# Latent queries, keys and values turned in one pair of transposes; latent keys and values in full-height passes over zero-padded weights

## The chip, the cores and the metric

The kernel runs on one core of one Trainium2 chip. The metric is the device time of one execution in microseconds (us); lower is better. One core has the engines PE (TensorE, matrix products, with its weight loads shown as a row of their own, PEld), DVE (VectorE), ACT (ScalarE), POOL (GpSimd) and SP (SyncE, which here only issues DMA transfers). PSUM, into which PE writes, has eight banks here, each holding 128 rows of 512 float32 values. All data are float32.

## The reference

One decoder layer for 8 sequences of 256 tokens and 256 channels, in three parts, each followed by a residual sum and a layer norm:

1. an attention with 16 heads and three branches, mixed by a gate per sequence. Its latent branch is what the change touches:
```python
nq  = _rms(x @ w_cq,  g_qnorm)        # 96 latent columns, for the queries
ckv = _rms(x @ w_ckv, g_kvnorm)       # 32 latent columns, for keys and values
q_nope, q_rope = nq @ w_dq_nope, rope(nq @ w_dq_rope)
k_nope = ckv @ w_dk_nope              # 16 heads x 32
v1     = ckv @ w_dv                   # 16 heads x 32
k_rope = rope(x @ w_krope) / 16       # shared by the heads
```
   The second branch attends to 64 selected tokens, the third to all tokens with keys and values made from `x` directly.
2. a cross attention with 16 heads over a context of 256 tokens;
3. eight experts of 1024 hidden units, of which a router weights two per token; all eight are computed.

## The kernel before

**The order of the work is planned when the program is built.** The kernel is written as 34 generators ("threads", lines 1436 to 1474), each of which yields operations. `Machine.run` (line 213) keeps for every engine the time at which it comes free, for every tile when it is written and read, and for every rotating buffer when it comes free. It takes from all threads the operation that can start earliest, and among those within 0.1 us the one of lowest rank. Each operation has an assumed cost (`mm` line 273: 2 x 0.00084 us per column, divided by `share` where several matmuls lie in different row groups; `dve_us`, `act_us`, `pool_us` lines 103 to 116). The result is a fixed order of instructions on each engine; the waits between engines follow from the data. So whatever changes an assumed cost, or the number of banks or buffers that an operation takes, can change the order of everything after it. The experts (`experts`, rank 99) are what PE does when nothing else is ready.

**PSUM** is eight tiles of one bank (`mtile`, line 308). A thread waits for a free one, or claims several at once (`m.claim`).

**The latents of a sequence** (`raw` line 744, `latents` line 758). `x` is multiplied with the 128 columns of `wA`: 96 for queries, then 32 for keys and values, into `lat` (tokens x latents). POOL squares it, DVE sums it per part, POOL makes the two reciprocal roots `rs`. DVE then scales the 96 query columns in place (line 779) and writes the 32 key-value columns twice side by side into `twice` (line 782). PE turns both, in two groups of two transposes (lines 789 and 790), into two halves of one PSUM bank, `plt`. DVE takes them out with the norm's gains: `lT` (96 rows, line 792) and `lk` (64 rows: the 32 latents in rows 0 to 31 and again in rows 32 to 63, line 793).

**Latent keys and values** (`latent_pairs`, line 924) come in two threads, "kn" and "vl", each twice per sequence, for two of the four head groups at a time. `wkv` holds the weights in 64 rows: rows 0 to 31 for the even head group, rows 32 to 63 for the odd one. A kn group is two matmuls of 32 rows x 256 columns, a vl group four of 32 rows x 128 columns; those of rows 0 to 31 and those of rows 32 to 63 lie in different row groups of the array and can run beside each other. Each head group has a PSUM bank of its own, so a group claims two. Each bank is copied out by itself (line 948, to `kn` or `vl`, by whichever of DVE and ACT the plan finds free first). `first` (line 974) multiplies queries with `kn`, `products` (line 1063) takes `vl` as weights.

**Other users of what the change touches.** `project` (line 843) uses `lT` for the queries. The two-buffer tag "turn" holds what the rotary embedding's multiply writes on DVE (`turn`, line 548) until POOL has read it; `twice` uses it too. `selection` (line 654) copies the selected tokens' values from PSUM to the tile `sv` (line 717) and writes it to DRAM. `setup` (line 382) issues the first loads on SP in order: inputs, `wA`, the rotary table, `gcol`, two loads of `gkv`, then four of `wkv`. `zeros` (line 430) clears tiles on POOL at the start.

Of the kernel before, what the change touches and what calls it, by code (L numbers as in the profile page):

```python
# [13 lines left out]
ALU = mybir.AluOpType  # L14
# [5 lines left out]
H = 16  # L20
# [238 lines left out]
def decoder_layer(ctx: ExitStack, tc: tile.TileContext, a: dict, out: bass.AP):  # L259
# [48 lines left out]
    def mtile(shape, name):  # L308
        return mtile_(shape, "m", name)

    def fixed(name, shape, dtype=F32):
        return const.tile(shape, dtype, tag=name, name=name)
# [38 lines left out]
    wkw = fixed("wkw", [P, 2, NHG, 3, HG * 32])  # L351
    wks = fixed("wks", [P, 2, NHG, 3, HG * 32])

    wkv = fixed("wkv", [64, 2, 2, P])
    gkv = fixed("gkv", [64, 1])
    wkr4 = fixed("wkr4", [P, 4, HG, 32])
    wo = fixed("wo", [P, 4, C])
    xWq = fixed("xWq", [P, 2, C])
# [23 lines left out]
    def setup():  # L382
        yield from load_sequence(0)
        yield dma(wA[:, :, 0:P], kp(a["w_lora"]))
        yield dma(wA[:, :, P:], kp(a["w_gi"]))
        done.add("first weights")
        wkr = two([P, 2, ROPE], "turn", "wkr")
        yield dma(wkr, kp(a["w_krope"]))
        for j in range(HG):
            yield dma(tab[bass.ts(j, 32)], a["rope"][0:32, 1])  # L390
        done.add("tab")
        yield dma(gcol, a["g_norm"])
        for n in range(2):
            yield dma(gkv[bass.ts(n, 32)], a["g_norm"][QL:P])
        done.add("inputs")
        yield V.tensor_scalar(
            wkr4,
            wkr.rearrange("p k (i r) -> p (k i) r", r=32).unsqueeze(2).to_broadcast([P, 4, HG, 32]),
            1.0 / H,
            None,  # L400
            ALU.mult,
        )
        m.release(wkr)
        yield seen("staged", 0)
        up = a["w_up"][QL:P, 0 : 2 * H * VH].rearrange("r (v g n c) -> n v r g c", v=2, n=2, c=P)
        for n in range(2):
            for v in range(2):
                yield dma(wkv[bass.ts(n, 32), :, v], up[n, v])
        done.add("latent weights")
        yield dma(wvw, kp(a["w_winv"]))  # L410
        yield dma(wvs, kp(a["w_selv"]))
        done.add("setup")
# [15 lines left out]
        m.release(t)  # L428

    def zeros():  # L430
        yield G.memset(vs[KEEP:P, 0], 0.0)
        yield G.memset(vs[0:KEEP, 1], 0.0)
        yield seen("heads", 0, 0)
        yield G.memset(vx, 0.0)
        yield G.memset(xk, 0.0)
        yield dma(wo, a["w_proj"].rearrange("(g p) c -> p g c", p=P))
        yield from compact(xWk, "xWk", 2)
        yield dma(xWv, kp(a["xWv"]))
        done.add("ctx weights")
        yield from compact(xWq, "xWq", 0)  # L440
        yield dma(mrow, a["xb"][:, 8:9])
        yield dma(bo, a["bo"].partition_broadcast(P))
        values = a["bv"].rearrange("(g i j d) -> j i d g", i=2, j=4, d=XH)
        rows = a["xWo"].rearrange("(g i j d) c -> j i d g c", i=2, j=4, d=XH)
        for j in range(4):
            for i in range(2):
                yield dma(wos[bass.ds(32 * j + XH * i, XH)], rows[j, i])
                yield dma(bv[bass.ds(32 * j + XH * i, XH)], values[j, i])
        yield V.tensor_scalar(qb, xb[:, 0:2], 0.25, None, ALU.mult)
        yield G.tensor_scalar(xq.rearrange("p g t -> p (g t)"), mrow.to_broadcast([P, NHG * T]), FILL, None, ALU.mult)  # L450

        wide = two([P, 2, P], "turn", "wide")
        yield G.tensor_copy(wide, bv.unsqueeze(2).to_broadcast([P, 2, P]))
        pb = mtile([P, C], "pbo")
        yield group([mm(pb, wide[:, g], wos[:, g], g == 0, g == 1) for g in range(2)])
        m.release(wide)
        yield V.tensor_tensor(bo, pb, bo, ALU.add)
        m.release(pb)
        done.add("query weights")
        yield dma(wr, kp(a["Wr"]))  # L460
        yield dma(br, a["br"].partition_broadcast(P))
        yield dma(b1, a["b1"])
        yield dma(b2, a["b2"])
        done.add("router weights")
# [189 lines left out]
    def selection(s, d):  # L654
# [59 lines left out]
            ]  # L714
        )
        used(lead(s))
        sv = one([P, H * VH], "sv", "sv")
        yield copied(sv[0:rows], pv[0:rows])
        m.release(pv)
        pro[lead(s)]["sv"] = dv = kept_in_dram([P, H * VH], f"sv{lead(s)}")  # L720
# [37 lines left out]
    def latents(s, d):  # L758
        xT = xTs[s]

        yield seen("raw", s)
        lat = d["lat"]
        sq = two([P, 2, P], "turn", "sq")
        yield G.tensor_tensor(sq, lat, lat, ALU.mult)
        ms = tiny("ms", [P, 2, 2])
        rs = tiny("rs", [P, 2, 2])
        parts = ((0, QL), (QL, P))
        for w, (lo, hi) in enumerate(parts):
            yield V.tensor_reduce(ms[:, w, :], sq[:, :, lo:hi], AX.X, ALU.add)
        m.release(sq)  # L770
        for w, (lo, hi) in enumerate(parts):
            yield V.tensor_scalar(ms[:, w, :], ms[:, w, :], 1.0 / (hi - lo), RMS_EPS, ALU.mult, ALU.add)
        yield rsqrt(rs.rearrange("p a b -> p (a b)"), ms.rearrange("p a b -> p (a b)"), 4)
        lT = one([P, T], "lT", "lT")
        lk = one([64, T], "lk", "lk")
        yield m.claim(lT, lk)
        yield seen("inputs")
        twice = two([P, 2, 2, 32], "turn", "twice")
        yield V.tensor_tensor(
            lat[:, :, 0:QL], lat[:, :, 0:QL], rs[:, 0, :].unsqueeze(2).to_broadcast([P, 2, QL]), ALU.mult  # L780
        )
        yield V.tensor_tensor(
            twice,
            lat[:, :, QL:P].unsqueeze(2).to_broadcast([P, 2, 2, 32]),
            rs[:, 1, :].unsqueeze(2).unsqueeze(3).to_broadcast([P, 2, 2, 32]),
            ALU.mult,
        )
        plt = mtile([P, 2, T], "plt")
        yield group([tr(plt[0:QL, 0, bass.ts(i, P)], lat[:, i, 0:QL]) for i in range(2)])
        yield group([tr(plt[0:64, 1, bass.ts(i, P)], twice[:, i].rearrange("p n c -> p (n c)")) for i in range(2)])  # L790
        m.release(lat, twice)
        yield V.tensor_scalar(lT[0:QL], plt[0:QL, 0], gcol[0:QL], None, ALU.mult)
        yield V.tensor_scalar(lk, plt[0:64, 1], gkv, None, ALU.mult)
        m.release(plt)
        d["lT"], d["lk"] = lT, lk
        done.add(("latent", s))
        lx = one([P, 2, T], "lx", "lx")
        yield m.claim(lx)
        pk = mtile([P, 2, T], "pkr")
        for i in range(2):  # L800
            yield group(
                [
                    mm(pk[:, i], wkr4[:, 2 * k + i].rearrange("p h r -> p (h r)"), xT[:, k, :], k == 0, k == 1)
                    for k in range(2)
                ]
            )
        yield from turn([lx[:, 0], lx[:, 1]], pk, T)
        m.release(pk)
        d["lx"] = lx
        done.add(("shared", s))  # L810
# [32 lines left out]
    def project():  # L843
        for s in range(B):
            yield 2 + AHEAD * s
            d = pro.setdefault(s, {})
            for g in range(NHG):
# [69 lines left out]
                )  # L917
                yield copied(h["vw"], pv)
                m.release(pv)
                if g == NHG - 1:  # L920
                    m.release(d["lT"])
                done.add(("values", s, g))

    def latent_pairs(name):

        for s in range(B):
            yield 2 + AHEAD * s
            d = pro.setdefault(s, {})
            for g in range(2):
                yield seen("heads", s, 2 * g)  # L930
                lk = d["lk"]
                t = one([P, 2, T], name, name)
                d[name, g] = t
                ps = [mtile([P, T], "p" + name) for _ in range(2)]
                yield m.claim(t)
                yield m.claim(*ps)
                ops = []
                for n, p_ in enumerate(ps):
                    rows = bass.ts(n, 32)
                    if name == "kn":  # L940
                        ops.append((p_, wkv[rows, g, 0], lk[rows]))
                    else:
                        ops += [(p_[:, bass.ts(i, P)], lk[rows, bass.ts(i, P)], wkv[rows, g, 1]) for i in range(2)]
                if name != "kn":
                    ops = ops[0::2] + ops[1::2]
                yield group([mm(*op, share=2) for op in ops], 0.1)
                for n, p_ in enumerate(ps):
                    yield copied(t[:, n], p_)
                m.release(*ps)
                done.add((name, s, g))  # L950
                if name != "kn" and g == 1:
                    yield seen("kn", s, 1)
                    m.release(lk)


    def scores(h, d, g, st, which):
# [106 lines left out]
    def products():  # L1063
        for s in range(B):
            yield 3 + AHEAD * s
            oT = None
            for g in range(NHG):
# [2 lines left out]
                yield seen("selected values", s)  # L1070
                yield seen("values", s, g)
                yield seen("vl", s, g // 2)
                vl = pro[s]["vl", g // 2][:, g % 2].rearrange("p (i c) -> p i c", i=2)
                if g == 0:
                    oT = one([P, NHG, T], "oT", "oT")
                    yield m.claim(oT)
# [494 lines left out]
```

## Time and profile before

| | |
|---|---|
| three timed runs | 1674.11, 1671.38, 1673.97 us; median 1673.97 |
| the profiled execution's own time | 1674.96 us |
| its span, first to last instruction | 1673.2 us |
| mean granted PE clock in it | 0.986 |
| busy: PE, PEld | 1609.5 us (96%), 1320.2 us (79%) |
| busy: DVE, ACT, POOL | 1158.9 (69%), 583.8 (35%), 599.7 us (36%) |
| HBM traffic | 196 GB/s over the span |

A float32 matmul appears as two PE rows (two passes), each with a weight load; a transpose as one. A PE row's duration is the time from its start to its modelled end, and successive passes overlap, so what a pass takes from PE is read from the distance of the starts of successive rows. A line of the timeline gives the start of a run of equal instructions, the time from the first start to the last end, and their number. A line of groups gives busy time, the mean duration of one in ns, and the idle time of the engine just before them with what ended it. In a line of the table of stages, each engine's busy time in the stretch is followed by its number of instructions, then the granted clock, the DMA share and GB/s.

### The profile page before, as it was taken

How to read it: one execution, taken by the hardware profiler on the slowest of the kernel's cores; microseconds unless marked ns; L12 is line 12 of the kernel's file. 1: busy time of each engine (PE TensorE's matmuls, PEld its weight loads, DVE VectorE, ACT ScalarE, POOL GpSimd, SP SyncE). 2: the span in 40 equal slices, each digit the busy share in tenths (PEclk: the TensorE clock that was granted, in tenths of full speed). 3: DMA queues.
4: the chain of work that ended last, by engine and by line, in shares of the span. 5: the costliest groups of instructions: out<-in, count | busy, mean ns of one | idle time of the engine just before them, and what ended most of it. 6: DMA issues, size and time to landing. Idle time of an engine off the chain costs nothing.

```text
span 1673.2 us, 31920 instructions
## 1 busy us (share of the span) xinstructions
PE 1609.5 (96%) x12040; PEld 1320.2 (79%) x12040; DVE 1158.9 (69%) x2577; ACT 583.8 (35%) x2114; POOL 599.7 (36%) x795
## 2 busy tenths in 40 slices
PE   6899789999999999999999999999999999999998
PEld 4778568887887778888888688878888778888887
DVE  4968678678789874887678884688767774544333
ACT  2464543244435430434434341244435341220000
POOL 3665753253534430334235332243335332120000
PEclk8999899999999999999999999999999999999999
DMA  6311416378648675655746676566656777585552
GB/s 218 117 50 47 166 69 217 120 245 284 233 141 291 245 248 192 211 205 189 252 172 234 241 249 227 151 238 211 226 196 221 248 257 251 154 307 153 161 156 96
DMA packets 185657, 329.96 MB, mean 197 GB/s; under 512 B 13200, under 2 KB 105504, under 8 KB 178336
## 3 DMA queue, kind: packets, MB, share of 16 engines
q1 hardware_dynamic: 185504, 327.92, 57.6%
q8 instruction: 96, 1.57, 0.4%
q14 instruction: 57, 0.47, 0.1%
HBM read 237.70 MB, written 90.19 MB: 196 GB/s over the span
## 4 chain that ended last, share of the span: by engine, by line
PE 83%; issue 7%; DVE 4%; DMA 3%; POOL 1%; SPq 1%; ACT 0%; POOLq 0%; DVEq 0%; ACTq 0%
PE ph L280 23%; PE py L280 22%; PE s L280 9%; PE o L280 4%; PE pk L280 3%; PE pyo L280 3%; PE ox L280 2%; PE pv L280 2%; PE sx L280 2%; DMA xpt<-prx 1%; PE pkm L280 1%; PE pks L280 1%; PE pq L280 1%; PE pt L286 1%; PE pkr L280 1%
## 5 line engine op out<-in xcount | busy, mean ns | idle before, releaser
L280 PE MATMUL ph<-xT,w 128*128 128x256 f32 x2048 | 475.2, 382 | 3.8 <-DVE pl L98 2.6
L280 PE MATMUL py<-w,h 128*128 128x256 f32 x2048 | 471.5, 381 | 0.0
L280 PEld LDWEIGHTS ph<-xT,w 128*128 128x128 f32 x2048 | 383.8, 190 | 70.2 <-issue 16.7
L280 PEld LDWEIGHTS py<-w,h 128*128 128x128 f32 x2048 | 383.7, 190 | 59.7 <-issue 7.7
L98 ACT ACTIVATE h<-ph,b 128x256 f32<-128x256 f32 x227 | 107.5, 473 | 391.5 <-PE ph L280 340.0
L98 DVE TENSOR_SCALAR h<-ph,b 128x256 f32<-128x256 f32 x285 | 136.9, 482 | 112.5 <-PE ph L280 109.6
L98 DVE SCALAR_TENSOR_TENSOR xr<-py,rw,xr 128x256 f32<-128x256 f32 x128 | 61.2, 478 | 174.7 <-PE py L280 174.6
L98 POOL TENSOR_TENSOR prx<-prx,sumsx 128x512 f32<-128x512 f32 x128 | 130.6, 1051 | 118.8 <-DVE sumsx L98 73.2
L98 ACT ACTIVATE prx<-sx,nmx 128x256 f32<-128x256 f32 x256 | 117.0, 486 | 43.3 <-DVE nmx L98 41.9
L98 POOL TENSOR_TENSOR pr<-pr,wpr 128x256 f32<-128x256 f32 (+2 forms) x128 | 129.4, 1042 | 0.0
L98 POOL TENSOR_TENSOR rstd<-var,nhalf 128x2 f32<-128x2 f32 x24 | 17.4, 725 | 310.0 <-DVE var L98 309.9
L98 ACT ACTIVATE pl<-pl,nmpl 128x128 f32<-128x128 f32 (+1 forms) x256 | 113.1, 446 | 30.6 <-DVE nmpl L98 29.9
L98 POOL TENSOR_TENSOR kx<-turn 128x64 f32<-128x64 f32 (+1 forms) x128 | 65.3, 527 | 162.6 <-DVE turn L98 156.9
L98 ACT ACTIVATE pr<-pr,nmpr 128x128 f32<-128x128 f32 (+1 forms) x256 | 113.2, 447 | 0.0
L98 DVE TENSOR_TENSOR pr<-s,causal 128x256 f32<-128x256 f32 x128 | 74.6, 583 | 41.0 <-PE s L280 34.6
L280 PE MATMUL s<-kx,q 32*128 32x320 f32 (+1 forms) x1536 | 96.1, 390 | 0.3 <-POOL kx L98 0.3
L98 POOL TENSOR_TENSOR pl<-pl,wpl 128x512 f32<-128x512 f32 x64 | 93.1, 1475 | 2.7
L98 POOL TENSOR_TENSOR q<-turn 128x256 f32<-128x256 f32 x64 | 45.8, 735 | 134.1 <-DVE turn L98 130.8
L280 PEld LDWEIGHTS s<-kx,q 32*128 32x128 f32 x1536 | 71.2, 189 | 17.8 <-issue 7.1
L98 DVE TENSOR_REDUCE nmx<-sx 128x2 f32<-128x512 f32 x128 | 79.1, 678 | 8.5 <-PE sx L280 8.5
L98 DVE TENSOR_TENSOR pl<-s,causal 128x256 f32<-128x256 f32 x128 | 74.3, 581 | 12.6 <-PE s L280 8.6
L98 DVE TENSOR_REDUCE nmpr<-pr 128x4 f32<-128x256 f32 (+2 forms) x128 | 80.5, 673 | 0.0
(217 smaller groups left out, 2385.1 us busy)
## 6 DMA issues: line engine op xcount, KB each, us to landing
w<-in_W SPq DMA_DIRECT2D x256, 512.0 KB, 4.2
pr<-pr SPq DMA_DIRECT2D x28, 1024.0 KB, 4.1
pa<-pr SPq DMA_DIRECT2D x28, 1024.0 KB, 6.9
prx<-prx SPq DMA_DIRECT2D x28, 1024.0 KB, 5.2
xpt<-prx SPq DMA_DIRECT2D x28, 1024.0 KB, 6.5
pl<-pl SPq DMA_DIRECT2D x28, 768.0 KB, 4.9
pb<-pl SPq DMA_DIRECT2D x28, 768.0 KB, 7.2
xT<-in_xT SPq DMA_DIRECT2D x8, 256.0 KB
```

The source lines that it names most:

```text
L98: return Op(self.name, us, outs, ins, lambda: getattr(self.engine, kind)(*args, **kw))
L280: lambda: nc.tensor.matmul(out, lhsT, rhs, start=start, stop=stop, skip_group_check=share > 1),
L286: return Op("PE", 0.11, [out], [in_], lambda: nc.tensor.transpose(out, in_, ident[:n, :n]), lag=0.17)
```

## The change

- `wkv` becomes 128 rows x 1024 columns (512 for keys, 512 for values). Rows 96 to 127 hold the weights and come in one DMA; rows 0 to 95 are cleared once by POOL at the start. `gkv` and its two DMAs go.
- In `latents`, the key-value columns are scaled in place like the query columns, without doubling; both are turned together, two transposes per sequence instead of four; one DVE instruction takes all 128 rows out with the gains of both. `lT` now has 128 rows, `lk` and `twice` go. `lT` is released in the "vl" thread, after the last use in `project`.
- In `latent_pairs`, each group is two matmuls of 128 rows x 256 columns into one bank: the 96 rows of query latents meet zeros. One copy of 512 columns takes the bank out. The tile is one bank where it was two, and is no longer claimed ahead.
- `sv` moves from a tile of its own to the "turn" buffers.
- `products` takes `vl` from its new layout.

```diff
--- before.py
+++ after.py
@@ -351,8 +351,7 @@
     wkw = fixed("wkw", [P, 2, NHG, 3, HG * 32])
     wks = fixed("wks", [P, 2, NHG, 3, HG * 32])
 
-    wkv = fixed("wkv", [64, 2, 2, P])
-    gkv = fixed("gkv", [64, 1])
+    wkv = fixed("wkv", [P, 2 * H * VH])
     wkr4 = fixed("wkr4", [P, 4, HG, 32])
     wo = fixed("wo", [P, 4, C])
     xWq = fixed("xWq", [P, 2, C])
@@ -390,8 +389,6 @@
             yield dma(tab[bass.ts(j, 32)], a["rope"][0:32, 1])
         done.add("tab")
         yield dma(gcol, a["g_norm"])
-        for n in range(2):
-            yield dma(gkv[bass.ts(n, 32)], a["g_norm"][QL:P])
         done.add("inputs")
         yield V.tensor_scalar(
             wkr4,
@@ -402,10 +399,7 @@
         )
         m.release(wkr)
         yield seen("staged", 0)
-        up = a["w_up"][QL:P, 0 : 2 * H * VH].rearrange("r (v g n c) -> n v r g c", v=2, n=2, c=P)
-        for n in range(2):
-            for v in range(2):
-                yield dma(wkv[bass.ts(n, 32), :, v], up[n, v])
+        yield dma(wkv[QL:P], a["w_up"][QL:P, 0 : 2 * H * VH])
         done.add("latent weights")
         yield dma(wvw, kp(a["w_winv"]))
         yield dma(wvs, kp(a["w_selv"]))
@@ -428,6 +422,7 @@
         m.release(t)
 
     def zeros():
+        yield G.memset(wkv[0:QL], 0.0)
         yield G.memset(vs[KEEP:P, 0], 0.0)
         yield G.memset(vs[0:KEEP, 1], 0.0)
         yield seen("heads", 0, 0)
@@ -714,7 +709,7 @@
             ]
         )
         used(lead(s))
-        sv = one([P, H * VH], "sv", "sv")
+        sv = two([P, H * VH], "turn", "sv")
         yield copied(sv[0:rows], pv[0:rows])
         m.release(pv)
         pro[lead(s)]["sv"] = dv = kept_in_dram([P, H * VH], f"sv{lead(s)}")
@@ -772,27 +767,18 @@
             yield V.tensor_scalar(ms[:, w, :], ms[:, w, :], 1.0 / (hi - lo), RMS_EPS, ALU.mult, ALU.add)
         yield rsqrt(rs.rearrange("p a b -> p (a b)"), ms.rearrange("p a b -> p (a b)"), 4)
         lT = one([P, T], "lT", "lT")
-        lk = one([64, T], "lk", "lk")
-        yield m.claim(lT, lk)
+        yield m.claim(lT)
         yield seen("inputs")
-        twice = two([P, 2, 2, 32], "turn", "twice")
-        yield V.tensor_tensor(
-            lat[:, :, 0:QL], lat[:, :, 0:QL], rs[:, 0, :].unsqueeze(2).to_broadcast([P, 2, QL]), ALU.mult
-        )
-        yield V.tensor_tensor(
-            twice,
-            lat[:, :, QL:P].unsqueeze(2).to_broadcast([P, 2, 2, 32]),
-            rs[:, 1, :].unsqueeze(2).unsqueeze(3).to_broadcast([P, 2, 2, 32]),
-            ALU.mult,
-        )
-        plt = mtile([P, 2, T], "plt")
-        yield group([tr(plt[0:QL, 0, bass.ts(i, P)], lat[:, i, 0:QL]) for i in range(2)])
-        yield group([tr(plt[0:64, 1, bass.ts(i, P)], twice[:, i].rearrange("p n c -> p (n c)")) for i in range(2)])
-        m.release(lat, twice)
-        yield V.tensor_scalar(lT[0:QL], plt[0:QL, 0], gcol[0:QL], None, ALU.mult)
-        yield V.tensor_scalar(lk, plt[0:64, 1], gkv, None, ALU.mult)
+        for w, (lo, hi) in enumerate(parts):
+            yield V.tensor_tensor(
+                lat[:, :, lo:hi], lat[:, :, lo:hi], rs[:, w, :].unsqueeze(2).to_broadcast([P, 2, hi - lo]), ALU.mult
+            )
+        plt = mtile([P, T], "plt")
+        yield group([tr(plt[:, bass.ts(i, P)], lat[:, i]) for i in range(2)])
+        m.release(lat)
+        yield V.tensor_scalar(lT, plt, gcol, None, ALU.mult)
         m.release(plt)
-        d["lT"], d["lk"] = lT, lk
+        d["lT"] = lT
         done.add(("latent", s))
         lx = one([P, 2, T], "lx", "lx")
         yield m.claim(lx)
@@ -917,8 +903,6 @@
                 )
                 yield copied(h["vw"], pv)
                 m.release(pv)
-                if g == NHG - 1:
-                    m.release(d["lT"])
                 done.add(("values", s, g))
 
     def latent_pairs(name):
@@ -928,29 +912,22 @@
             d = pro.setdefault(s, {})
             for g in range(2):
                 yield seen("heads", s, 2 * g)
-                lk = d["lk"]
+                lT = d["lT"]
                 t = one([P, 2, T], name, name)
                 d[name, g] = t
-                ps = [mtile([P, T], "p" + name) for _ in range(2)]
-                yield m.claim(t)
-                yield m.claim(*ps)
-                ops = []
-                for n, p_ in enumerate(ps):
-                    rows = bass.ts(n, 32)
-                    if name == "kn":
-                        ops.append((p_, wkv[rows, g, 0], lk[rows]))
-                    else:
-                        ops += [(p_[:, bass.ts(i, P)], lk[rows, bass.ts(i, P)], wkv[rows, g, 1]) for i in range(2)]
-                if name != "kn":
-                    ops = ops[0::2] + ops[1::2]
-                yield group([mm(*op, share=2) for op in ops], 0.1)
-                for n, p_ in enumerate(ps):
-                    yield copied(t[:, n], p_)
-                m.release(*ps)
+                p_ = mtile([P, 2, T], "p" + name)
+                if name == "kn":
+                    yield group([mm(p_[:, n], wkv[:, bass.ts(2 * g + n, P)], lT) for n in range(2)])
+                else:
+                    w = wkv[:, bass.ds(H * VH + 2 * P * g, 2 * P)]
+                    yield group([mm(p_[:, i], lT[:, bass.ts(i, P)], w) for i in range(2)])
+                yield copied(t, p_)
+                m.release(p_)
                 done.add((name, s, g))
-                if name != "kn" and g == 1:
-                    yield seen("kn", s, 1)
-                    m.release(lk)
+            if name == "vl":
+                yield seen("kn", s, 1)
+                yield seen("values", s, NHG - 1)
+                m.release(lT)
 
 
     def scores(h, d, g, st, which):
@@ -1070,7 +1047,7 @@
                 yield seen("selected values", s)
                 yield seen("values", s, g)
                 yield seen("vl", s, g // 2)
-                vl = pro[s]["vl", g // 2][:, g % 2].rearrange("p (i c) -> p i c", i=2)
+                vl = pro[s]["vl", g // 2][:, :, bass.ts(g % 2, P)]
                 if g == 0:
                     oT = one([P, NHG, T], "oT", "oT")
                     yield m.claim(oT)
```

## The prediction

> **What bounds the kernel.** I read the page's busy shares first, then the table of stages, then PE's waits, then PE's timeline around the groups that change.
>
> ```profile
> PE 1609.5 (96%) x12040; PEld 1320.2 (79%) x12040; DVE 1158.9 (69%) x2577; ACT 583.8 (35%) x2114; POOL 599.7 (36%) x795
> ...
> PE 83%; issue 7%; DVE 4%; DMA 3%; POOL 1%; SPq 1%; ACT 0%; POOLq 0%; DVEq 0%; ACTq 0%
> ```
>
> PE is busy for 96% of the span and is 83% of the chain that ended last. The stages show where the rest is:
>
> ```profile
> 0.00:40.00 40.00, 24.05 (x122) 18.35 (x126) 17.85 (x54) 7.77 (x18) 15.09 (x33) 0.83 0.68 212
> 40.00:80.00 40.00, 35.32 (x310) 29.61 (x302) 36.95 (x104) 17.45 (x61) 26.38 (x41) 0.91 0.44 138
> 80.00:160.00 80.00, 76.17 (x793) 60.95 (x792) 63.70 (x159) 45.14 (x155) 50.37 (x63) 0.98 0.14 48
> 160.00:310.00 150.00, 133.94 (x1161) 106.36 (x1160) 110.53 (x263) 66.56 (x250) 72.93 (x96) 0.94 0.44 155
> 310.00:1673.00 1363.00, 1340.06 (x9667) 1104.97 (x9666) 929.86 (x2000) 446.87 (x1634) 434.94 (x562) 1.00 0.62 212
> ```
>
> In the first 310 us PE is busy for 269.5 and idle for 40.5; its clock is below 1.00 there, which costs about 0.17 x 40 + 0.09 x 40 + 0.02 x 80 + 0.06 x 150 = 21 us more. Afterwards it is idle for 22.9 us in 1363, about 6.6 of it after its last matmul. So after 310 us each added us of PE's time is an added us of the kernel; before, it is partly a matter of who waits.
>
> **The price of a pass.** The last experts give it without disturbance:
>
> ```profile
> 1569.71 7.07 PE L280 MATMUL ph<-xT,w 128*128 128x256 f32 x32
> 1576.62 0.59 PE L280 MATMUL py<-w,h 128*128 128x256 f32 x2
> ```
>
> From start to start 6.91 us for 32 passes: 0.216 us for a pass of 128 rows and 256 columns. pq, with 96 rows, has a mean duration of 394 ns against 382 for ph: I count a full-height pass at 0.216 whatever its rows. A new group, kn or vl, is 2 matmuls x 2 passes x 0.216 = **0.864 us**.
>
> **The price of the groups that go.** A kn and a vl group between full-height neighbours, and a kn group behind scores, which are in row groups themselves:
>
> ```profile
> 1236.44 0.38 PE L280 MATMUL pq<-lT,wq 96*128 96x256 f32 x1
> 1236.75 0.70 PE L280 MATMUL pkn<-lk,wkv 32*128 32x256 f32 x4
> ...
> 1237.38 1.99 PE L280 MATMUL ph<-xT,w 128*128 128x256 f32 x8
> ```
>
> ```profile
> 820.82 0.28 PE L280 MATMUL pv<-wvw,xT 128*128 128x128 f32 x1
> 821.03 0.71 PE L280 MATMUL pvl<-wkv,lk 32*128 32x128 f32 x8
> ...
> 821.67 0.48 PE L280 MATMUL ph<-xT,w 128*128 128x256 f32 x1
> ```
>
> ```profile
> 1147.30 0.61 PE L280 MATMUL s<-kn,q 32*128 32x256 f32 x8
> 1147.73 0.60 PE L280 MATMUL pkn<-lk,wkv 32*128 32x256 f32 x4
> 1148.26 1.56 PE L280 MATMUL py<-w,h 128*128 128x256 f32 x6
> ```
>
> From pq's last pass to ph it is 0.94 us; without the group it would be 0.216, so the kn group costs 0.724. The vl group costs 0.85 - 0.112 (a 128-column pass) = 0.737. Both hold a changeover: the step into row groups takes 0.309 where a pass takes 0.216. Behind scores that changeover is paid anyway (row groups to full height, median 0.304 from start to start), and the kn group costs 0.73 - 0.304 = 0.42.
>
> I went through all 32 groups in this way, by their neighbours:
> - 8 kn and 10 vl groups between full-height work: 8 x 0.140 + 10 x 0.127 = +2.4 us.
> - 3 kn groups behind scores, one between two sorts of partial passes: 4 x 0.44, less 0.02 = +1.7.
> - 2 vl groups behind column-group work (cost 0.643): 2 x 0.22 = +0.4. 2 vl groups just ahead of scores (0.45): 2 x 0.42 = +0.8.
> - Twice a kn and a vl group in a row beside scores: +0.62 and +0.65 = +1.3.
> - 2 kn groups that stalled (377 and 710 us), at the clean difference: +0.3.
> Sum **+7.0 us** (0.22 a group). If the new plan put every group between full-height work it would be 32 x 0.13 = +4.3; if beside scores, 32 x 0.44 = +14.
>
> The Trainium skill's page "TensorEngine Tiling (Array Packing)", section "Theoretical Speedup", promises up to twice the speed for a contraction of at most 64 rows, and speaks against this change: by it the groups would have cost half of 0.864, and the change would add 32 x 0.432 = 13.8 us where I have 7.0. The trace has 0.724 and 0.737 between full-height work, so I keep the rows.
>
> **Transposes.** 16 of them go, at half the distance here:
>
> ```profile
> 1216.22 0.38 PE L286 MATMUL plt<-ident,twice 128*64 128x128 f32 x2
> 1216.44 1.46 PE L280 MATMUL py<-w,h 128*128 128x256 f32 x6
> ```
>
> 0.22 us for two, 8 x 0.22 = **-1.75 us**. The remaining ones grow from 96 to 128 weight columns: their loads are 127 ns against 190 for a full one, beside a neighbour's pass; nothing counted (at most 16 x 0.06 = 1 us).
>
> **Stalls of the two-bank groups.** The kn group at 377 us took 1.65 us from its first start to the next work where 0.63 is normal; the one at 710 had its second bank late:
>
> ```profile
> 710.05 0.59 PE L280 MATMUL pkn<-lk,wkv 32*128 32x256 f32 x2
> 711.39 0.66 PE L280 MATMUL pkn<-lk,wkv 32*128 32x256 f32 x2 [0.75 <-DVE pr L98]
> ```
>
> Together 2.5 us over the clean cost. With one bank there is one wait in place of two, which may be as late. I take **-1.0**, bounds 0 and -2.5.
>
> **The start.** At 11.4 us PE waits for `lat`, then turns both halves for 0.88 us before pkr. The new order waits for the second scaling as well (about 0.1 us later: `twice` starts 0.27 after `lat`, and its half-size successor is shorter), then needs only 0.43. pkr comes 0.35 us sooner, DVE's multiply waits for it, and the top-k chain behind it on DVE holds up PE until 26.8 (6.67 us). SP drops two gkv and three wkv issues of about 0.47 us ahead of the next staged weights, 2.3 us, but those wait for buffers and the chain for DVE. I take **-0.4**, bounds 0 and -1.0.
>
> **Costed at nothing.**
> - DVE loses `lk` (0.47 us) and part of `twice`, 8 times: some 5 us of 1159, beside PE's work. It can only help.
> - Copies: two of 256 columns (0.38 each on ACT, 0.41 on DVE) become one of 512 (0.585 and 0.68). The first scores with the keys wait for it; two in a row on ACT took 0.65, so it lands no later. If both copies had run beside each other it lands 0.2 later; at worst 32 x 0.3 = 10 us, if PE had nothing else, but experts stand ready from about 250 us.
> - The clearing of `wkv`: a clear of 128 x 1024 took POOL 0.95 us; POOL sits idle for 4.64 us before 7.75. If it came later, one 0.95 us in front of `sq` would move the whole start by that.
> - `sv` in a "turn" buffer: five copies (36.7, 97.5, 303.4, 706.6, 1090.3 us), held until the write has landed, 3 us. The nearest multiply behind them comes 6.9, over 9, 7.4, over 9 and 8.7 us later. None waits in this order; in another, behind a held buffer, up to 3 us of DVE each, at most 15, which PE mostly fills.
> - `lT`'s release moves threads but has the same conditions: the next latents waited for `lk` at the same point.
>
> **The new plan.** Cheaper latents, dearer groups and half the banks change the assumed costs, so the order changes from the first sequence on. No row shows by how much. Its field is the early idle time and lost clock, 40.5 + 21 us; a fifth of the 40.5 either way, 8 us, is my bound, and its value 0, because PE's work after 310 us is full in any order.
>
> **Sum:** +7.0 - 1.75 - 1.0 - 0.4 = **+3.9 us**. Against the profiled execution's 1674.96 that is 1678.8; it lies 1.0 above the median of the runs, so I state 1674.0 + 3.9 = about **1678**.
>
> **Rivals.**
> - **Within 0.2%** (3.35 us, about what a measurement of this kernel can tell from no change). Both credits come at their ends: 7.0 - 1.75 - 2.5 - 1.0 = +1.75, **1676**. For it: the stalls are in the trace. Against: one bank can be as late as two.
> - **Faster**, by one mechanism: the early plan. A pair of groups holds one bank where it held two, and DVE has a latent step less in front of `turn`, just where PE idles for DVE (the longest waits there are 6.7 for the top-k chain, 5.2 for a layer norm, 2.7 for `lat`). If a fifth of the 40.5 + 21 us goes, -12, with +5.2 paid in passes: -7, **1667**. It decides from 3.9 + 3.35 = 7.3 us gained, an eighth of the field. Against: the two longest waits have nothing in them that the change removes.
> - **Slower by more.** The new order opens one more hole like the one at 243 us, 5.2 us for a layer norm, followed by 6.8 us at half clock (3.4 lost): 1678 + 8.6 = **1687**.
> - **The groups don't cost what I say**: were the passes not bound by their columns but by the 32 useful rows, nothing would be added and the sum would be -3, 1671. pq at 96 rows against ph at 128, 394 and 382 ns, speaks against it; it is counted with the faster case.
>
> **Chances.** Forecast 0.40; within 0.2% 0.27; slower by more 0.13; faster 0.20 (0.03 of it for the last rival). So slower by over 0.2%: 0.53, same 0.27, faster 0.20. The range takes in the bound of the plan on both sides, 1678 + 8 and somewhat more for the hole, and most of the faster case: **1667 to 1687**.
>
> **What will show it.** pkn and pvl as 4 passes each, 0.216 apart, 0.86 from start to next start, with no 0.309 step before; two plt transposes a sequence; PE busy time up by 4 to 6 us; the stage from 310 us on as full as before. I am wrong if the groups stand at another distance, or if the first 310 us differ by more than 8 us.

## The result, and the profile after

| | before | after |
|---|---|---|
| median of the timed runs | 1674.04 us (4 runs) | 1697.47 us (4 runs) |
| ratio, 95% interval | | 1.0145, 1.013 to 1.016 |
| span of the profiled execution | 1673.2 us | 1694.7 us |
| PE busy / idle (span less busy) | 1609.5 / 63.7 us | 1623.2 / 71.5 us |
| mean granted PE clock | 0.986 | 0.981 |

The kernel became slower by 23 us, as forecast in sign, but by six times the forecast 3.9 and outside the range. Because the median of the kernel before varied from 1672.4 to 1675.1 us between the groups of runs below, I compare by ratios, each against runs of the kernel before in the same group; 0.0010 of ratio is 1.7 us.

**A new group costs what was forecast.** PE's timeline of the kernel after, a kn and a vl group between full-height passes:

```profile
1261.26 1.03 PE L280 MATMUL pkn<-lT,wkv 128*128 128x256 f32 x4
1262.12 1.03 PE L280 MATMUL pq<-lT,wq 96*128 96x256 f32 x4
1262.99 1.03 PE L280 MATMUL pvl<-wkv,lT 128*128 128x256 f32 x4
1263.85 0.81 PE L280 MATMUL py<-w,h 128*128 128x256 f32 x3
```

Each is 4 passes and 0.86 us from its start to the next start, and pq with 96 rows takes as long. The transposes came down to two a sequence, 0.22 us for the pair:

```profile
1235.83 0.38 PE L286 MATMUL plt<-ident,lat 128*128 128x128 f32 x2
1236.05 1.68 PE L280 MATMUL py<-w,h 128*128 128x256 f32 x7
```

**The rest is idle time and clock.** The same table of stages as before the change (PE's busy time is the second figure, the clock the third from the end):

```profile
0.00:40.00 40.00, 23.93 (x117) 17.84 (x118) 17.61 (x54) 7.42 (x17) 16.33 (x34) 0.83 0.69 211
40.00:80.00 40.00, 35.75 (x295) 30.13 (x296) 35.28 (x103) 16.55 (x55) 26.74 (x41) 0.91 0.47 139
80.00:160.00 80.00, 78.05 (x843) 62.91 (x841) 64.94 (x167) 50.87 (x176) 48.82 (x64) 1.00 0.12 41
160.00:310.00 150.00, 127.80 (x1058) 100.39 (x1051) 116.46 (x257) 60.82 (x226) 75.99 (x96) 0.91 0.39 135
310.00:1695.00 1385.00, 1357.66 (x9660) 1123.52 (x9658) 935.26 (x1988) 442.11 (x1607) 440.24 (x569) 0.99 0.63 211
```

Up to 160 us nothing is lost. From 160 to 310 PE is idle for 22.2 us where it was 16.1, at a clock of 0.91 where it was 0.94. From 310 on it is idle for 27.3 where it was 22.9, at 0.99 where it was 1.00. Over the whole span the clock's loss (span times what is missing to 1) is 32.2 us against 23.4. While PE idles a low clock costs nothing, so I count half of PE's busy time in the stretches at half clock: 24.5 us against 15.9. So of the span's +21.5 us, 7.8 are idle time, 8.6 the clock, and what is left, about 5, is busy time of another kind: dearer passes and whatever else PE's order adds.

The two longest new holes, in PE's timeline:

```profile
215.88 1.51 PE L280 MATMUL o<-pb,vl 128*32 128x128 f32 x16 [5.89 <-DMA pb<-pl]
...
563.25 1.51 PE L280 MATMUL o<-pa,vw 128*32 128x256 f32 x16 [7.50 <-ACT prx L98]
```

By the profile, the first waits for a transfer, the second for ACT to read scores out of their PSUM bank. ACT in its turn waited for DVE, whose timeline shows what stood in front of the reduction that ACT needed:

```profile
557.51 1.41 DVE L98 TENSOR_TENSOR_SCAN sc<-left 1x256 f32<-1x256 f32 x1
558.95 1.08 DVE L98 TENSOR_TENSOR sc<-sc,left 1x256 f32<-1x256 f32 x1
560.07 1.01 DVE L98 TENSOR_SCALAR sc<-sc 1x256 f32<-1x256 f32 x1
...
561.32 2.48 DVE L98 TENSOR_REDUCE nmx<-sx 128x2 f32<-128x512 f32 x4
```

That is the top-k chain of another sequence. None of these DVE instructions is touched by the change; only their place in the order is new.

### The profile page after: what moved, and what is told of

It is laid out like the page before. It is cut to its first block, busy times and chain, and to the rows that moved or that the text cites. A ratio compares the mean times of both kernels' runs of the same rounds, so it can differ in the third digit from the quotient of the medians.

```text
span 1694.7 us, 31673 instructions
## 1 busy us (share of the span) xinstructions
PE 1623.2 (96%) x11960; PEld 1334.8 (79%) x11960; DVE 1169.5 (69%) x2565; ACT 577.8 (34%) x2079; POOL 608.1 (36%) x803
## 4 chain that ended last, share of the span: by engine, by line
PE 79%; DVE 7%; issue 7%; DMA 4%; POOL 2%; ACT 0%; SPq 0%; POOLq 0%; DVEq 0%; ACTq 0%
PE ph L280 22%; PE py L280 21%; PE s L280 9%; PE o L280 3%; PE pk L280 3%; PE pyo L280 2%; PE pv L280 2%; PE sx L280 2%; PE ox L280 2%; PE pq L280 2%; PE pks L280 2%; PE pkm L280 1%; DMA pb<-pl 1%; DMA pl<-pl 1%; DVE left L98 1%
## 5 line engine op out<-in xcount | busy, mean ns | idle before, releaser
L280 PE MATMUL ph<-xT,w 128*128 128x256 f32 x2048 | 480.0, 383 | 0.3 <-PE o L280 0.2
L98 DVE TENSOR_SCALAR h<-ph,b 128x256 f32<-128x256 f32 x314 | 150.5, 482 | 115.2 <-PE ph L280 112.5
L98 ACT ACTIVATE h<-ph,b 128x256 f32<-128x256 f32 x198 | 94.0, 475 | 361.8 <-PE ph L280 361.3
```

The source lines that it names most:

```text
L98: return Op(self.name, us, outs, ins, lambda: getattr(self.engine, kind)(*args, **kw))
L280: lambda: nc.tensor.matmul(out, lhsT, rhs, start=start, stop=stop, skip_group_check=share > 1),
```

## The theories

**Theory A: the removed claim.** The change also drops a line that the prediction passed over: `latent_pairs` no longer claims its destination tile (`kn`, `vl`: one buffer each) before the matmuls. The vl group of 174 us is the clearest case, in PE's and in ACT's timeline:

```profile
174.36 1.03 PE L280 MATMUL pvl<-wkv,lT 128*128 128x256 f32 x4
```

```profile
217.45 0.59 ACT L98 COPY vl<-pvl 128x512 f32<-128x512 f32 x1 [0.31 <-PE o L280]
```

The product lies in its PSUM bank for 43 us, until `vl` is free. Added over all groups (first matmul to end of copy, times banks), latent groups hold banks for 584 us; it was 110. By theory A the lost bank makes the holes.

**Theory B: the order.** The change alters assumed costs, the number of banks and the claims, so the planner arranges everything anew. The order of the kernel before is better than most; the new one is just another.

**Theory D**, added after the first runs: the change's instructions cost more than their passes (operands later, `sv` in the "turn" buffers).

## Experiments: claims, costs, banks

**e1**, the change with its claim put back:

```diff
                 p_ = mtile([P, 2, T], "p" + name)
+                yield m.claim(t)
```

> The changed kernel with one line added: latent_pairs claims its destination tile (kn or vl) before it issues the matmuls, as the kernel before did. Theory A (a latent group that is multiplied before its destination tile is free keeps its PSUM bank for up to 90 us, and that lost bank makes the new holes): the loss beyond the dearer passes goes, about 16 us, time 1677 to 1682, pvl banks held about 1.7 us each in place of 31 on average. Theory B (any change of assumed costs gives a different and, by chance, worse order): the time stays within some 8 us of 1697 or goes anywhere.

Measured: 1.0135 (1.0114 to 1.0156), 1696.3 us. Latent groups hold banks for only 54 us in total, yet PE is idle for 81.3 us. Theory A misses: the claim alone brings back nothing that can be told from the change (1.0145).

**e2**, the kernel before without it:

```diff
-                yield m.claim(t)
                 yield m.claim(*ps)
```

> The kernel before with one line removed: latent_pairs no longer claims its destination tile ahead (the two banks are still claimed). No instruction differs in kind or number. Theory A: pairs of banks are held for tens of us and the kernel slows by at least the 16 us seen in the changed kernel, which holds one bank, not two: 1688 to 1710. Theory B: an order that differs by chance, within 8 us of 1674.

Measured: 1.0288 (1.0255 to 1.0321), 1721.8 us. Banks are held for 1068 us. This alone would suit theory A.

**e3**, the change with the old assumed cost:

```diff
-yield group([mm(p_[:, n], wkv[:, bass.ts(2 * g + n, P)], lT) for n in range(2)])
+yield group([mm(p_[:, n], wkv[:, bass.ts(2 * g + n, P)], lT) for n in range(2)], -0.33)
...
-yield group([mm(p_[:, i], lT[:, bass.ts(i, P)], w) for i in range(2)])
+yield group([mm(p_[:, i], lT[:, bass.ts(i, P)], w) for i in range(2)], -0.33)
```

> The changed kernel with the planner told that a latent group costs 0.53 us, as it was told before, in place of 0.86; the instructions are the same in kind and number. Theory A: banks are held as in the changed kernel, 1690 to 1702. Theory B, in the form that the dearer assumed cost spoiled the order: back to 1677 to 1682.

Measured: 1.0278 (1.0249 to 1.0307), 1721.1 us. Neither: it is 22 us above the change, with banks held as long (593 us). A cost told closer to the old one made the order worse.

**e4**, the kernel before with seven banks:

```diff
-    mtile_ = m.pool(ps, 8)
+    mtile_ = m.pool(ps, 7)
```

> The kernel before with 7 PSUM tiles in place of 8: the price of one bank missing all the time. In the changed kernel latent groups hold a bank for 584 us in total (sum over 32 groups), against some 110 before. Theory A: if 470 us of one bank cost 16 us, a bank missing for the 1400 us in which attention runs costs up to 50: 1690 to 1724. Theory B: the eighth bank is worth little, within 8 us of 1674.

Measured: 1.0207 (1.0186 to 1.0228), 1708.3 us, inside theory A's bounds. But by now everything that was altered had cost 23 to 48 us, whatever it was. That called for two other kinds of run: one that changes the order and nothing else, and one that changes everything but the order.

## Experiments: the order alone, and everything but the order

**j1 and j2**: the kernel before, instruction for instruction, with one assumed cost altered.

```diff
-                yield group([mm(*op, share=2) for op in ops], 0.1)
+                yield group([mm(*op, share=2) for op in ops], 0.12)
```

> The kernel before with the planner told that a latent group costs 0.02 us more (0.55 in place of 0.53). Not an instruction differs in kind or number; the order is the same up to about 300 us. Theory B, with the order of before a rare good one: 1680 to 1710. If plans scatter evenly about 1674: within 8 us of it on either side. Theories A and D: 1674, since no bank is held and nothing is added.

```diff
-.get(kind, 0.15 + 0.00106 * n)
+.get(kind, 0.151 + 0.00106 * n)
```

> The kernel before with the planner told that every plain VectorE instruction costs 0.001 us more. Not an instruction differs in kind or number; the order differs from about 60 us on. Theory B: 1680 to 1720. Theories A and D: 1674.

Measured: j1 1.0135 (1.0113 to 1.0158), 1698.4 us; j2 1.0189 (1.0162 to 1.0216), 1707.1 us. Nothing was added, latent groups hold banks no longer than before (96 us each), and the loss is about as large as the change's or larger. j1's stages, of which the first 300 us have the old order:

```profile
160.00:310.00 150.00, 132.87 (x1147) 105.62 (x1149) 108.97 (x256) 65.16 (x243) 73.00 (x96) 0.93 0.44 152
310.00:1703.00 1393.00, 1355.49 (x9684) 1114.01 (x9672) 953.37 (x2017) 438.32 (x1618) 442.33 (x569) 0.98 0.62 208
```

The scores that start at 304.2 us in the kernel before start at 305.7 here, 1.5 us later; the whole span is 29.3 us longer. After 310 us PE is idle for 37.5 us (22.9 before) and the clock is at 0.98. Over the whole span PE's idle time grew by 15.3 us and the clock's loss while PE is busy by 13.8 (29.7 against 15.9), which together make the 29.

**j3**: as j2, downwards (0.149).

> The kernel before with the planner told that every plain VectorE instruction costs 0.001 us less; no instruction differs in kind or number. Theory B, order of before a rare good one: 1685 to 1715, like the two others. If orders scatter evenly about 1674, this is the one that should come out below it.

Measured: 1.0119 (1.0092 to 1.0145), 1693.8 us. Three altered orders, all slower by 20 to 32 us: the order of the kernel before is no middle of its scatter.

**x1 and x2**: the change in the old order. The planner's picks for the kernel before (which thread, on which engine) were recorded and imposed on the changed kernel:

```diff
-            t, _, op, th = min(picks, key=lambda x: x[0])
+            who, engine = divmod(order.pop(), 5)
+            th = next(th for th in threads if th[3] == who)
+            ops = th[2] if isinstance(th[2], tuple) else (th[2],)
+            op = next(o for o in ops if o.engine == names[engine])
```

x1 keeps two banks and two copies per group:

> The changed kernel's latents, weights and full-height passes, but with the two banks, the two copies and the claims of the kernel before, and with every engine's instructions in the recorded order of the kernel before (only what the change removes is left out of it; vl in 8 passes of 128 columns, 0.112 us each). Theory A, now in doubt: nothing to lose here, 1678 to 1681. Theory B (the plan's order is the loss, not any instruction): 7.0 + 0.5 - 1.75 = +5.8, so 1678 to 1681. Theory D (the change's own instructions cost more than their passes: later operands, sv in the turn buffers): 1688 or more.

x2 is the whole change but for the claims: the destination tile is claimed again, and a second bank is claimed and left unused.

```diff
-                p_ = mtile([P, 2, T], "p" + name)
+                p_, spare = mtile([P, 2, T], "p" + name), mtile([P, T], "spare")
+                yield m.claim(t)
+                yield m.claim(p_, spare)
```

> All of the change (one bank per group, one copy, sv in the turn buffers), with every engine's instructions in the recorded order of the kernel before. The destination tile is claimed ahead and a second, unused bank is claimed with the group, so that the claims fall where they fell. Theory B: +5.2 for passes and transposes, less the stalls, 1676 to 1681. Theory D: 1688 or more.

Measured: x1 1.0030 (1.0016 to 1.0044), x2 1.0029 (1.0012 to 1.0045), 1679.7 and 1679.5 us. The change, in the old order, costs 4.9 us (2.0 to 7.5). From x2's table of stages:

```profile
160.00:310.00 150.00, 134.11 (x1149) 107.32 (x1152) 110.39 (x258) 67.74 (x250) 74.80 (x98) 0.94 0.45 156
310.00:1679.00 1369.00, 1343.94 (x9634) 1112.02 (x9623) 929.11 (x1995) 446.97 (x1618) 435.47 (x562) 1.00 0.62 211
```

Idle time and clock are close to those of the kernel before: 15.9 us at 0.94 and 25.1 at 1.00, where it had 16.1 and 22.9. Theory D falls. Theory B holds: same instructions, old order +5, new order +24. Since x2 also claims its destination tile, the strictest comparison is with e1, which does so too: 1.0029 in the old order, 1.0135 in a new one, 18 us for the order alone.

**d1**: x2 with each latent group multiplied twice.

```diff
-yield group([mm(p_[:, n], wkv[:, bass.ts(2 * g + n, P)], lT) for n in range(2)])
+yield group([mm(p_[:, n], wkv[:, bass.ts(2 * g + n, P)], lT) for n in range(2)] * 2)
```

> The change in the order of the kernel before (as x2), with every latent key and value group multiplied twice over into the same bank: 128 full-height passes more, 0.216 us each, and the order of no engine altered. If PE is the bound wherever these groups stand: 1679.5 + 27.6 = 1707. If half of them fell into time in which PE waits anyway: about 1693. It prices a pass in place, and with it the term +7.0 - 1.75 of the prediction.

Measured: 1.0185 (1.0156 to 1.0213), 0.0156 above x2: 26 us for the expected 27.6. PE's busy lines of x2 and of d1:

```profile
PE 1612.0 (96%) x11960; PEld 1327.8 (79%) x11960; DVE 1155.4 (69%) x2561; ACT 582.9 (35%) x2090; POOL 601.0 (36%) x796
```

```profile
PE 1639.4 (96%) x12088; PEld 1352.0 (80%) x12088; DVE 1155.6 (68%) x2561; ACT 583.1 (34%) x2090; POOL 601.2 (35%) x796
```

128 passes more, 27.4 us more of busy time, 0.214 each: the passes lie on the path that sets the end.

## Experiments: is the claim worth anything?

Since orders scatter, one run each way can't tell. The same two alterations (0.151 and 0.149) gave more draws of the change (k1, k2), of the change with its claim (c1, c2) and of the kernel before without it (c3, c4).

> The changed kernel with the planner told that every plain VectorE instruction costs 0.001 us more. Theory B: another draw of the same scatter as the order of before with the same alteration (1707) or the claimed and re-costed versions of the change (1696, 1721): 1690 to 1725. If the change itself spoiled the order by its structure, its draws lie above those of the kernel before by more than the 5 us of its passes.

> The changed kernel with the planner told that every plain VectorE instruction costs 0.001 us less. As for the alteration upwards: 1690 to 1725 by theory B, its mean with the others above that of the altered orders of the kernel before by about 5 us.

> The changed kernel with the destination tile claimed ahead (as e1), and the planner told that a plain VectorE instruction costs 0.001 us more. If held banks cost, the draws with the claim (1696 and these two) lie below those without it (1697, 1721, 1716, 1704; mean 1710) by 10 us or more. If they cost nothing that shows, this is one more draw from 1690 to 1722.

> As the run with 0.001 us more, with 0.001 us less: below 1700 on average with the two others if held banks cost; 1690 to 1722 if not.

> The kernel before without the claim of the destination tile (as e2), and the planner told that a plain VectorE instruction costs 0.001 us more. If pairs of banks held for tens of us cost, the draws without the claim (1722 and these two) lie above those with it (1698, 1707, 1694; mean 1700) by some 20 us. If not: 1690 to 1722, mean near 1700.

> As the run with 0.001 us more, with 0.001 us less: about 1720 on average with the two others if held banks cost; near 1700 if not.

| draws | ratios to the kernel before | mean | banks held by latent groups |
|---|---|---|---|
| before, altered (j1, j2, j3) | 1.0135, 1.0189, 1.0119 | 1.0148 | 93 to 96 us |
| before, no claim (e2, c3, c4) | 1.0288, 1.0190, 1.0409 | 1.0296 | 961 to 1217 us |
| change with claim (e1, c1, c2) | 1.0135, 1.0118, 1.0138 | 1.0130 | 54 to 58 us |
| change (after, e3, k1, k2) | 1.0145, 1.0278, 1.0249, 1.0177 | 1.0212 | 467 to 629 us |

The intervals are about 0.002 to 0.003 either way, for c1 to c4 (fewer timed runs) 0.0035 to 0.008. Without the claim the mean is higher by 0.0148 (25 us) in the kernel before and by 0.0082 (14 us) in the change. With three or four draws each, which spread by 0.002 to 0.022, this points to a price of going without the claim, on the average over orders; that the held bank is the reason is argued, not shown, since every draw is also another order. Nor does it show a price for the particular order of the changed kernel, which lies only 0.0010 above e1. And between the change with its claim and the altered orders of the kernel before there is no difference at all (1.0130, 1.0148): the 5 us that the change costs in the old order drown in the scatter.

## Why the prediction was right in sign and wrong in size

- **Price of a pass, and transposes, -1.75**: right. The new groups stand 0.86 us apart, the pairs of transposes 0.22, and d1 prices a pass at 0.214 busy.
- **Price of the groups that go, in the +7.0**: too low between full-height work, so the term was some 2 us too large. I took 0.724 and 0.737 us, up to the start of the first pass behind the group. But where row groups end, the second full-height pass comes 0.320 us after the first, not 0.216 (76 cases, 0.319 to 0.321), which I passed over. The kernel before and x2 have the same work around a kn group:

```profile
1235.69 1.13 PE L280 MATMUL pq<-lT,wq 96*128 96x256 f32 x4
1236.75 0.70 PE L280 MATMUL pkn<-lk,wkv 32*128 32x256 f32 x4
1237.38 2.86 PE L280 MATMUL ph<-xT,w 128*128 128x256 f32 x12
1240.17 0.73 PE L280 MATMUL s<-lx,q 32*128 32x128 f32 x16
```

```profile
1241.00 1.13 PE L332 MATMUL pq<-lT,wq 96*128 96x256 f32 x4
1241.97 1.03 PE L332 MATMUL pkn<-lT,wkv 128*128 128x256 f32 x4
1242.84 2.75 PE L332 MATMUL ph<-xT,w 128*128 128x256 f32 x12
1245.52 0.73 PE L332 MATMUL s<-lx,q 32*128 32x128 f32 x16
```

From pq to the scores it is 4.48 us before and 4.52 in x2: +0.04 where I had +0.140. By the starts in the two traces, the vl groups between full-height work give +0.025 where I had +0.127. For these 18 groups that is about +0.5 us in place of +2.4, and the whole term about +5. Behind scores, my +0.44 is what the traces show.

- **Stalls of the two-bank groups, -1.0 (0 to -2.5)**: in x2 the group at 379 us takes 0.89 us from its start to the next work's, the one at 713 takes 1.20; they were 1.65 and 1.94. Less the clean costs some 2 us of stalls went, near the far end of my bounds.
- **The start, -0.4**: not there. From PE's first instruction to the end of the top-k wait it is 21.67 us before and after, and 22.3 in x2, where DVE's `lat` came later.
- **Costed at nothing** (copies, clearing of `wkv`, `sv` in "turn", `lT`): a few us at most. x1 and x2, with two copies and one, differ by 0.0001, and in the old order all of the change together costs 4.9 us; none of these was tested by itself.
- **These terms together, +3.9**: x2's +4.9 (2.0 to 7.5) lies close, but partly by luck. With the sizes measured above they come to 5 - 1.75 - 2 = about +1.3. In the profiled executions x2's span is 5.7 us longer, of which 3.2 are idle time and 1.6 the clock's loss while PE is busy, which leaves about 1. The interval begins at 2.0, so part of that idle time and clock seems to belong to x2 itself; where it comes from, no run shows.
- **The new plan, 0, at most 8 us either way**: this is the step that failed. It was about +19: the change lies 0.0116 above x2, the same work in another order and without the claim (0.0106, 18 us, for e1 with it). So of the 24 us measured, some 19 came from a term that I had set at nothing. Two things were wrong in it. I took its field to be the first 310 us, "because PE's work after 310 us is full in any order"; j1 has the old order until about 300 us and loses nearly all of its 29 us behind it. PE was full there because the order was good: in the changed kernel PE stands idle for 7.50 us ahead of `o` at 563.25 us, and the experts' next pass, `ph` at 567.30, stands behind it in the order. And I set the value to 0, as if an order were as likely to be better as worse; all thirteen altered kernels that were planned anew lie 20 to 68 us above the kernel before, none below. The field was also smaller than the 40.5 + 21 us that I named: of the 41 us at half clock in the first 310, PE was idle for 12, so the clock cost about 14 there, not 21.
- **The claim**: I listed its removal in the change and counted only the banks ("half the banks"), not how long one is held: 43 us in the case shown. The draws point to a price on average; in this order it isn't separable.
- **Rivals**: the mechanism of "slower by more" (one more hole of 5.2 us and the half clock behind it) was the right one; there were several, so 9 us was too little. "Faster" rested on DVE's relief and on freed banks in the early stage; DVE was busy for 10.6 us more after the change (in the new order it does 314 of the experts' copies `h` where it did 285), and PE's idle time rose.
- **Signs**: the groups' distance came as said. PE's busy time rose by 13.7 us where I named 4 to 6, and the stage from 310 us on was less full: the two signs that speak of the order.

What stays open: what makes the order of the kernel before so good, and which of the new order's holes carry how much of its loss. Against x2 the span is 15.8 us longer, of which 4.6 are idle time and 7.0 the clock's loss while PE is busy; some 4 us of busy time I can't assign. No version here beats the kernel before.

## What to carry to other kernels

Where a planner orders a program, price the change's instructions and the new order as two terms. The second can be measured without the change, by altering an assumed cost by a thousandth of a microsecond: if that alone moves the time by 20 us, a step of 5 us can't be judged from one build, and has to be run in the recorded old order. A claim that holds a producer back until its consumer's buffer is free looks like a cost; dropping it lets the product sit in a scarce bank (43 us in the case shown), and it is worth a test of its own. And where a group changes the array's shape, its price is read up to where the passes behind it run at their usual distance again, not to the first of them.

## What the runs showed of the hardware

A latent group in two groups of 32 rows, between full-height work, costs hardly less than the same product over 128 rows, three quarters of them zeros: about 0.83 us (kn) and 0.84 (vl) against 0.864. The step into row groups took 0.309 us, the step out 0.304 (median), and the second pass behind it came 0.320 after the first, where full-height passes stand 0.216 apart. Beside scores, which are in row groups already, a kn group cost 0.42, half of 0.864. The Trainium skill's page "TensorEngine Tiling (Array Packing)", section "Key Properties", says that a change of the tiling mode drains the engine, which agrees; the factor of two in its section "Theoretical Speedup" was reached beside other row groups, and not for groups as short as these between full-height work.

Around the two long new holes of the changed kernel, of 5.89 us up to 215.88 and of 7.50 us up to 563.25, the clock was lost as well. The stages:

```profile
215.00:221.80 6.80, 5.92 (x37) 5.08 (x38) 1.52 (x4) 2.13 (x4) 3.93 (x4) 0.50 0.21 78
...
559.70:566.50 6.80, 3.25 (x48) 2.17 (x48) 6.73 (x11) 3.76 (x16) 1.24 (x2) 0.50 0.02 4
```

Both times the granted clock was 0.50 for 6.8 us. In the first, PE was busy for 5.92 us of them, so about 3.0 us were lost on top of the hole; in the second, half of the stretch lay in the hole itself, and about 1.6 us were lost. In the first of these stretches eight transposes took 1.91 us from the first start to the last end; in the kernel before, at full clock, eight took 1.04:

```profile
219.93 1.91 PE L286 MATMUL pt<-ident,prx 128*128 128x128 f32 x8
```

```profile
229.83 1.04 PE L286 MATMUL pt<-ident,prx 128*128 128x128 f32 x8
```
